# Second attention's sums: four engines in written order, its token states made beside the scans, routing cut into stages

## The chip, the core and the metric

The kernel runs on one core of a Trainium2 chip. A core has five engines that run side by side, each through its own queue in order: PE (TensorE, matrix products into PSUM), DVE (VectorE), ACT (ScalarE), POOL (GpSimd, which also issues the indirect DMAs here) and SP (which issues other DMAs). They wait for each other through semaphores. The metric is the device time of one execution in microseconds; lower is better.

## What is computed

Four layers work on an image of 256 channels and 64x64 points. Layers 0 and 1 are a windowed linear attention and a deformable convolution. The change is in layer 2, which sees the image as 4096 tokens of 256 channels: a gated linear attention over the tokens with 8 heads of 32 channels, and then a mixture of experts in which each token goes to its two best of eight. Layer 3 has a softmax attention and another such mixture. What matters of layer 2, cut:

```python
t = t + _L2_attn_ref(_ln_t(t), ...)
t = t + _L2_ffn_ref(_ln_t(t), ...)

# in _L2_attn_ref
sim = jnp.einsum('bhld,bhld->bhl', q, k) * qk_norm_scale
k = _l2_normalize(k)
v = _l2_normalize(v)
Z = jnp.einsum('bhld,bhle->bhlde', v, k) * kv_norm_scale
gates_logits = jnp.einsum('bhli,oi->bhlo', gate_inputs, wg_w) + wg_b
gates = jnp.square(jax.nn.relu(gates_logits)) + EPS
m_scan, s_scan = _online_softmax_scan(sim)
Z_scan = jnp.cumsum(gates[..., None] * Z, axis=2)
g_scan = jnp.cumsum(gates[..., None], axis=2)
softmax_weights = (jnp.exp(sim - m_scan) / (s_scan + EPS))[..., None, None]
attn_weights = Z_scan / (g_scan + EPS) * (1.0 + jax.nn.silu(softmax_weights))
ctxt = jnp.einsum('bhld,bhlde->bhle', q, attn_weights)
return _linear(ctxt, wo_w, wo_b)

# in _moe, on the normalized tokens
probs = jax.nn.softmax(tokens @ router_w.T, axis=-1)
rw, re = jax.lax.top_k(probs, TOP_K)
```

## The kernel before

All is in 32-bit floats, and the 4096 tokens are 32 tiles of 128 (`NT`; `P` is 128, `C` 256, `D` 32, `NB` 512, `TPB` 4). `attn2` holds queries and keys in `A["qk"]`, values in `A["v"]` and their transposes in `A["vT"]`, and goes through three stages.

**Projections** (`attn2_project`): layer norm, queries, keys and values, gates, and keys scaled by their gates (L1507 on POOL), block by block of four tiles.

**Scans** (`attn2_fac`): the running sums and maxima along the tokens, as one factor per token and head. They are a chain of small steps on DVE and ACT; `carry` twice sends ends of segments through PE (`c8`, then `back`). They end in `A["fac"]`.

**Sums** (`attn2_sum`): 16 slots of two tiles. In slot u, `turn(u+1)` transposes the next scaled queries (PSUM tag "o", copied to `qT` by ACT), `states(u)` makes the products of values and keys of its two tiles (128x128 each, of which the 32x32 blocks on the diagonal are used) and adds them to the running state on DVE, `out(u-1)` multiplies the context by the output weights (tag "o" too) and adds it to the tokens `t` on DVE, `context(u)` adds what earlier tiles give (`earlier`, L1655, with the state) and what the tile itself gives (`within`, L1661), and `scores(u+1)` makes the next scores, which DVE masks with the triangle (L1631). `scale(u)` on POOL multiplies the queries by the factor and adds the bias `wo_b` to the tokens (L1609, L1610).

Between these, every second slot starts `route` for four finished tiles, a generator in five pieces: layer norm; transposes; the second transposes and t = t (1 + r) + shift on ACT (L1970); logits, the two best experts (`top2`) and counts; places and eight scatters (L2006, indirect DMAs on POOL, one for each tile and rank) of the normalized rows into the experts' lists `xs` in DRAM. After the last of them `tile_table` works out which expert each tile of the lists belongs to, and `expert_tiles` loads weights and rows (L2095 to L2102).

The order: in the sums only PE's order is as written (`manual_schedule` with PE alone). Those of DVE, ACT and POOL are set when the program is built, by a planner that follows priorities and its own idea of when each input is there; so the 16 additions of L1610 run during the projections already, and the 16 of L1609 at the start of the sums. In the scans the planner sets all engines. The square root in `layer_norm` (L204) and the exponential in `top2` (L1941) use different tables of ACT, which loads a table ahead of the first function that needs another one.

## Time and profile before

| what | us |
|---|---|
| median of 10 runs | 3437.05 (3431.53 to 3440.94) |
| profiled execution | 3435.9 |
| its span, first to last instruction | 3433.7 |
| mean granted clock of PE | 0.955 |
| projections of layer 2 | 1436 to 1567 |
| scans | 1567 to 1586 |
| sums: first scaled query to end of the last context | 1586.0 to 1725.2 |
| last scatter issued | 1757.3 |
| first load of expert weights | 1760.3 |

Times in the trace count from the span's start. A group's row gives busy time and mean length of one instruction, and then how long the engine was idle just before it, with what released it. In the timeline, a row merges equal instructions that follow each other, and stands at the start of the first.

In the projections DVE is busy 119.3 of 131 us and PE 117.0. From 1763 on the experts follow, and then layer 3, which ends at 3433.7; the change leaves their code as it is.

### The profile page before, as it was taken

Reading aid. Unit: us, or ns where it says so; the run is one execution under the profiler, and the core shown is the slowest. Engines: PE = TensorE matmul, PEld = TensorE weight load, DVE = VectorE, ACT = ScalarE, POOL = GpSimd, SP = SyncE. Lnnn points to the kernel's source line nnn. Section 1 sums busy time; section 2 is a strip of 40 time slices with the busy share of each in tenths; the row PEclk is TensorE's granted clock in tenths of the full one; section 3 lists DMA queues with packets and bytes.
Section 4 is the critical chain, followed back from the end, with each engine's and each line's share of the span. In section 5 each row is a group of like instructions: output and inputs, shape, how many; then the busy total and the mean of one; then the engine's idle time right before and its main releaser. Section 6 shows DMA issues by size and latency. Waiting matters only on the chain.

```text
span 3433.7 us, 65430 instructions
## 1 busy us (share of the span) xinstructions
PE 3100.0 (90%) x25404; PEld 2322.7 (68%) x25404; DVE 2309.3 (67%) x5378; ACT 1318.8 (38%) x2538; POOL 1448.4 (42%) x1293
## 2 busy tenths in 40 slices
PE   6779999999977899897969699999999996999997
PEld 3443444344435888665857468888888885989896
DVE  8885677577754677797755576777777775555552
ACT  4444344444425666243533352222222222333331
POOL 2028788788833555343444352000000003555552
PEclk9889999999989999898979899999999997999998
DMA  2145556521133222100158643322333314555554
GB/s 72 42 115 144 161 155 168 127 68 52 49 119 109 68 71 73 47 1 1 63 178 267 216 181 120 102 89 93 99 99 101 96 56 160 194 196 208 202 202 175
DMA packets 241686, 406.97 MB, mean 119 GB/s; under 512 B 78353, under 2 KB 152850, under 8 KB 231890
## 3 DMA queue, kind: packets, MB, share of 16 engines
q1 hardware_dynamic: 212002, 344.40, 32.2%
q0 software_dynamic: 13056, 35.93, 2.8%
q10 hardware_dynamic: 16304, 22.31, 1.9%
q8 instruction: 204, 3.34, 0.4%
q14 instruction: 120, 0.98, 0.1%
HBM read 287.07 MB, written 111.30 MB: 116 GB/s over the span
## 4 chain that ended last, share of the span: by engine, by line
PE 41%; DVE 9%; DMA 5%; issue 5%; ACT 3%; POOL 3%; SPq 0%; DVEq 0%; POOLq 0%; ACTq 0%
PE a_sa_ps L2438 6%; PE f_h_ps L146 5%; DMA ys<-f_y,f_at 3%; PE l_acc_ps L1132 3%; PE a_oa_ps L2477 3%; PE a_ob_ps L2477 3%; PE a_oc_ps L2477 3%; PE a_sb_ps L2438 3%; PE f_ya_ps L146 2%; PE f_yb_ps L146 2%; DVE l_pr L1128 2%; PE a_od_ps L2477 1%; POOL ys L2193 1%; PE a_sc_ps L2438 1%; PE a_q_ps L146 1%
## 5 line engine op out<-in xcount | busy, mean ns | idle before, releaser
L748 ACT COPY l_sc<-l_s 128x384 f32<-128x384 f32 (+1 forms) x632 | 303.9, 532 | 454.3 <-PE l_s L741 448.0
L753 DVE TENSOR_TENSOR l_sm<-l_s,mask 128x256 f32<-128x256 f32 (+2 forms) x628 | 308.0, 551 | 91.7 <-PE l_s L741 90.6
L2006 POOL DMA_INDIRECT xs<-f_room,f_to x64 | 64.7, 1012 | 696.7 <-issue 581.5
L146 PE MATMUL f_h_ps<-f_xT,f_w 128*128 128x256 f32 x1440 | 340.7, 387 | 18.9 <-DVE f_xT L2113 9.5
L146 PEld LDWEIGHTS f_h_ps<-f_xT,f_w 128*128 128x128 f32 x1440 | 262.1, 192 | 82.8 <-ACT f_h L2123 31.5
L741 PE MATMUL l_s<-l_q,l_k 32*128 32x256 f32 (+3 forms) x2944 | 270.5, 453 | 0.0
L2457 ACT ACTIVATE a_e<-a_e 128x512 f32<-128x512 f32 x256 | 155.8, 629 | 242.3 <-DVE a_e L2427 241.3
L758 POOL TENSOR_TENSOR l_sm<-l_sc,mask 128x768 f32<-128x768 f32 (+1 forms) x116 | 203.0, 1758 | 88.1 <-ACT l_sc L748 87.9
L2123 ACT ACTIVATE f_h<-f_h_ps,f_w 128x256 f32<-128x256 f32 x360 | 166.4, 470 | 187.6 <-PE f_h_ps L146 178.0
L1128 DVE TENSOR_TENSOR l_pr<-l_vk,l_w_ps 128x1280 f32<-128x1280 f32 x128 | 186.6, 1481 | 56.9 <-PE l_acc_ps L1132 38.4
L741 PEld LDWEIGHTS l_s<-l_q,l_k 32*128 32x128 f32 x2944 | 132.4, 183 | 115.2 <-issue 67.2
L1132 PE MATMUL l_acc_ps<-ident,l_pr 128*128 128x128 f32 x1600 | 198.8, 278 | 7.7 <-POOL l_pr L1123 7.6
L2193 POOL DMA_INDIRECT ys<-f_y,f_at x144 | 145.8, 1013 | 138.1 <-ACT f_y L2192 108.0
L1132 PEld LDWEIGHTS l_acc_ps<-ident,l_pr 128*128 128x128 f32 x1600 | 185.3, 144 | 14.2 <-POOL l_pr L1123 8.6
L762 POOL TENSOR_TENSOR l_sm<-l_sc,mask 128x256 f32<-128x256 f32 (+1 forms) x220 | 185.2, 871 | 14.1 <-ACT l_sc L748 13.3
L2150 POOL TENSOR_TENSOR f_wt<-f_w 128x512 f32<-128x512 f32 x72 | 90.0, 1270 | 218.5 <-PE f_ya_ps L146 207.1
L2438 PE MATMUL a_sa_ps<-a_q,a_kt 128*128 128x256 f32 x512 | 155.9, 386 | 13.7 <-DVE a_u L2443 12.9
L2442 ACT COPY a_u<-a_sa_ps 128x256 f32<-128x256 f32 x128 | 47.6, 372 | 293.4 <-PE a_sa_ps L2438 293.4
L787 PE MATMUL l_b_ps<-l_sm,l_v 128*32 128x256 f32 (+2 forms) x2176 | 153.7, 372 | 0.0
L2438 PE MATMUL a_sa_ps<-a_qt,a_kt 128*128 128x256 f32 x512 | 153.1, 381 | 0.0
L758 POOL TENSOR_TENSOR l_sm<-l_sc,mask_c 128x768 f32<-128x768 f32 (+1 forms) x64 | 120.9, 1905 | 40.4 <-ACT l_sc L748 39.9
L2438 PE MATMUL a_sb_ps<-a_qt,a_kt 128*128 128x256 f32 x512 | 131.4, 379 | 0.0
(559 smaller groups left out, 7274.9 us busy)
## 6 DMA issues: line engine op xcount, KB each, us to landing
a_kt<-a_kd SPq DMA_DIRECT2D x128, 512.0 KB
f_w<-in_f_w SPq DMA_DIRECT2D x36, 1152.0 KB
f_w<-in_f_w SPq DMA_DIRECT2D x36, 1028.0 KB
xs<-zero SPq DMA_DIRECT2D x8, 4160.0 KB
l_vk<-vt SPq DMA_DIRECT2D x180, 128.0 KB
f_x<-xs SPq DMA_DIRECT2D x72, 260.0 KB
f_w<-in_f_w SPq DMA_DIRECT2D x36, 384.0 KB
l_rcp<-l_recd SPq DMA_DIRECT2D x48, 256.0 KB
```

What stands on the lines that cost most here:

```text
L146: self.nc.tensor.matmul(out, lhsT, rhs, start=(i == 0), stop=(i == len(pairs) - 1))
L741: nc.tensor.matmul(s[pair, j][:, at : at + m, :], key(hp), qs[hp], start=(z == 0), stop=(z == len(pieces) - 1))
L748: nc.scalar.copy(sc[:, j], s[1, j])
L753: nc.vector.tensor_tensor(to(pair, j, kind, at), pick(s[pair, j], kind, which), mask, ALU.mult)
L758: nc.gpsimd.tensor_tensor(out[:, :, at, :], of[:, :, which, :], bc(mask, 1, 2), ALU.mult)
L762: nc.gpsimd.tensor_tensor(to(1, j, kind, at), pick(sc[:, j], kind, which), mask, ALU.mult)
L1128: nc.vector.tensor_tensor(pr, vk, bc(held["w"][:, j, dy], 3, D), ALU.mult)
L1132: nc.tensor.matmul(acc[:, m, j, :], pf[:, dx, m * P : (m + 1) * P], self.ident, is_transpose=True, start=(j == 0 and dy == 0 and dx == 0 a ...
L2123: nc.scalar.activation(h[:, m, :], q, AF.Gelu, bias=w1[:, 2 * hidden + m : 2 * hidden + m + 1])
L2193: nc.gpsimd.indirect_dma_start(out=self.ys_parts[(i % 4) * NI + k], in_=y[:, k, :], in_offset=None, out_offset=bass.IndirectOffsetOnAxis(a ...
L2438: mm = lambda out, i, right: nc.tensor.matmul(out, A[i], right, start=True, stop=True)
L2477: nc.tensor.matmul(out, vs[:, j, i, :], right, start=(j == 0 and side != 1), stop=(j == NPAIR - 1 and side != 0))
```

## The change

The token states go from the sums to the scans. `attn2_states` makes, for each of the first 31 tiles, eight products of 128x32 by 128x32 (four heads in each half), so that only the 32x32 blocks are made; ACT copies four tiles at a time from PSUM to `A["st"]`, and POOL adds them up one after the other. `beside(n)` writes n tiles of these ahead of PE's `c8`, `back` and last transposes in the scans (8, 1, 12, 1 and the remaining 9 tiles). The scans are reordered: the running maximum and its exponentials come ahead of the sum of the gates, and the reciprocal of that sum is written at the end.

In the scans and in the sums PE, DVE, ACT and POOL now all run in written order. `scale` and the addition of `wo_b` are two steps, `scale(u+2)` and `bias(u+1)` of a slot. `route` is cut into 14 named steps by `route_parts` (`norm_parts` cuts the layer norm); for the sums `do(u, late, name)` writes a step `late` slots after that in which its group's last tiles are finished, and scatters go out four to a slot. The last four tiles are two groups of two. The transposed queries and the context lie in the projection weights' room `w_qkv2`, whose use is over, the triangle is made before the projections, and the PSUM bank of the states becomes one for logits and places ("few"). The steps of routing themselves are the same as before; `route` for layer 3 runs them in its old order.

```diff
@@ -1361,6 +1383,7 @@
+            tri = self.triangle(pool)
...
+            left = ExitStack()
+            A["st"] = left.enter_context(tc.tile_pool(name="a2s", bufs=1)).tile([P, NT, 2, D], F32, tag="st", name="a2_st")
             self.attn2_fac(A)
...
-                bank = lambda: ps.tile([P, NB], F32, tag="r", name="f_r_ps")
+                bank = lambda few=False: ps.tile([P, TPB * NE if few else NB], F32, tag="few" if few else "r", name="f_r_ps")
...
-                    return self.route(t0, T, t, S, wp, n.rearrange("p (i c) -> p i c", c=CX), nT, bank)
-                self.attn2_sum(t, A, ked, wp, ps, route)
+                    return self.route_parts(t0, T, t, S, wp, n.rearrange("p (i c) -> p i c", c=CX), nT, bank)
+                self.attn2_sum(t, A, tri, ked, wp, ps, route)
+    def attn2_states(self, A, ps):
+        nc = self.nc
+        st, banks = A["st"], []
+        def product(ti):
+            if ti % 8 == 0:
+                banks.append(ps.tile([P, 8, 2, D], F32, tag=f"st{ti // 8}", name="a2_st_ps"))
+            for m in range(2):
+                for h in range(4):
+                    hp, at = slice(h * D, (h + 1) * D), slice(m * P + h * D, m * P + (h + 1) * D)
+                    nc.tensor.matmul(banks[-1][hp, ti % 8, m, :], A["v"][:, ti, at], A["qk"][:, ti, C + at.start : C + at.stop], start=True, stop=True)
+            if ti % 4 == 3 or ti == NT - 2:
+                lo = ti // 4 * 4
+                nc.scalar.copy(st[:, lo + 1 : ti + 2], banks[-1][:, lo % 8 : ti % 8 + 1])
+                for i in range(max(1, lo), ti + 1):
+                    nc.gpsimd.tensor_tensor(st[:, i + 1], st[:, i + 1], st[:, i], ALU.add)
+        return [(lambda ti: lambda: product(ti))(ti) for ti in range(NT - 1)]
     def attn2_fac(self, A):
...
+            tc.manual_schedule(engines={ET.PE, ET.DVE, ET.Activation, ET.Pool}),
...
+            states = self.attn2_states(A, ps)
+            def beside(n):
+                for go in states[:n]:
+                    go()
+                del states[:n]
...
+            def carry(ends, scan, first, fill):
...
                 p = ps.tile([NH, len(ends), NS], F32, tag="c8", name="a2_c8")
+                beside(fill)
                 self.mm(p.rearrange("p j s -> p (j s)"), [(hot, R.rearrange("p j s -> p (j s)"))])
...
                 p = ps.tile([P, len(first), NS], F32, tag="back", name="a2_back")
+                beside(1)
                 self.mm(p, [(hotT, x[:, :, 0:NS])])
...
-            c2 = carry([ends[:, 0:1], ends[:, 1:2]], sums_and_tops, (0.0, -3e38))
+            c2 = carry([ends[:, 0:1], ends[:, 1:2]], sums_and_tops, (0.0, -3e38), 8)
+            mx = pool.tile([P, L + 1], F32, tag="mx", name="a2_mx")
+            nc.vector.tensor_copy(mx[:, 0:1], c2[:, 1:2])
+            nc.vector.tensor_tensor_scan(mx[:, 1:], s, s, c2[:, 1:2], ALU.max, ALU.max)
+            far = pool.tile([P, L], F32, tag="far", name="a2_far")
+            nc.scalar.activation(far, mx[:, 1:], AF.Exp, scale=-1.0, bias=c2[:, 1:2])
+            nc.vector.tensor_sub(s, s, mx[:, 1:])
+            nc.scalar.activation(s, s, AF.Exp)
+            dec = pool.tile([P, L], F32, tag="dec", name="a2_dec")
+            nc.vector.tensor_sub(dec, mx[:, :L], mx[:, 1:])
+            nc.scalar.activation(dec, dec, AF.Exp)
             gs = pool.tile([P, L], F32, tag="gs", name="a2_gs")
             nc.vector.tensor_tensor_scan(gs, one.to_broadcast([P, L]), g, c2[:, 0:1], ALU.mult, ALU.add)
             nc.vector.tensor_scalar_add(gs, gs, 1e-5)
-            mx = pool.tile([P, L + 1], F32, tag="mx", name="a2_mx")
-            nc.vector.tensor_copy(mx[:, 0:1], c2[:, 1:2])
-            nc.vector.tensor_tensor_scan(mx[:, 1:], s, s, c2[:, 1:2], ALU.max, ALU.max)
-            nc.vector.tensor_sub(s, s, mx[:, 1:])
-            dec = pool.tile([P, L], F32, tag="dec", name="a2_dec")
-            nc.vector.tensor_sub(dec, mx[:, :L], mx[:, 1:])
-            far = pool.tile([P, L], F32, tag="far", name="a2_far")
-            nc.scalar.activation(s, s, AF.Exp)
-            nc.scalar.activation(dec, dec, AF.Exp)
-            nc.scalar.activation(far, mx[:, 1:], AF.Exp, scale=-1.0, bias=c2[:, 1:2])
             tot = pool.tile([P, L], F32, tag="tot", name="a2_tot")
             nc.vector.tensor_tensor_scan(tot, dec, s, 0.0, ALU.mult, ALU.add)
             c1 = carry([tot[:, L - 1 : L], far[:, L - 1 : L]],
                        lambda x, c: nc.vector.tensor_tensor_scan(x[:, 0, :], c[:, 1, :], c[:, 0, :], 0.0, ALU.mult, ALU.add),
-                       (0.0,))
+                       (0.0,), 12)
...
             nc.vector.reciprocal(gs, gs)
             nc.vector.scalar_tensor_tensor(s, s, 1.0, gs, ALU.add, ALU.mult)
+            beside(len(states))
             p = ps.tile([P, 2, P], F32, tag="fac", name="a2_fac_ps")
...
-    def attn2_sum(self, t, A, ked, wp, ps, route):
+    def attn2_sum(self, t, A, tri, ked, wp, ps, route):
...
-        tri = self.triangle(wp)
-        qTs, sms, before, cTs = {}, {}, {}, {}
+        ET = mybir.EngineType
+        U = NT // 2
+        qTs, sms, cTs, R = {}, {}, {}, {}
+        room = lambda i: w["w_qkv2"].rearrange("p k n -> p (k n)")[:, i * NB : (i + 1) * NB].rearrange("p (m j n) -> p m j n", m=2, j=2)
         two = lambda u: slice(2 * u, 2 * u + 2)
         keys = lambda ti: A["qk"][:, ti, C:]
         def scale(u):
             qh = A["qk"][:, two(u), 0:C].rearrange("p t (h d) -> p t h d", d=D)
             nc.gpsimd.tensor_tensor(qh, qh, bc(A["fac"][:, :, u, :], 3, D), ALU.mult)
+        def bias(u):
             nc.gpsimd.tensor_tensor(t[:, two(u), :], t[:, two(u), :], bc(self.row("wo_b"), 1, 2), ALU.add)
...
-            qTs[u] = wp.tile([P, 2, 2, P], F32, tag="qT", name="a2_qT")
+            qTs[u] = room(u % 2)
...
-        def states(u):
...
-                        nc.tensor.matmul(c[hp, m, j, :], before[2 * u + j][hp, m, hp], qTs[u][hp, m, j, :], start=(first and m == 0), stop=False)
+                        nc.tensor.matmul(c[hp, m, j, :], A["st"][hp, 2 * u + j, m, :], qTs[u][hp, m, j, :], start=(first and m == 0), stop=False)
...
-            cTs[u] = wp.tile([P, 2, 2, P], F32, tag="cT", name="a2_cT")
+            cTs[u] = room(2)
...
-        steps = []
...
-        with self.tc.manual_schedule(engines={mybir.EngineType.PE}):
-            scale(0)
-            scale(1)
+        groups = [(2 * r + 2, 4 * r, 4) for r in range(U // 2 - 1)] + [(U - 1, NT - 4, 2), (U, NT - 2, 2)]
+        def do(u, late, name, *args, only=(4, 2)):
+            for at, t0, T in groups:
+                if at + late == u and T in only:
+                    if t0 not in R:
+                        R[t0] = route(t0, T)
+                    if args and isinstance(args[0], slice):
+                        R[t0][name](range(T)[args[0]])
+                    else:
+                        R[t0][name](*args)
+        every, fore, hind = slice(None), slice(0, 2), slice(2, 4)
+        with self.tc.manual_schedule(engines={ET.PE, ET.DVE, ET.Activation, ET.Pool}):
+            for u in range(2):
+                scale(u)
+            bias(0)
             turn(0)
             scores(0)
-            for u in range(U + 1):
+            for u in range(U + 7):
+                if u + 1 < U:
+                    turn(u + 1)
+                do(u, 1, "norm")
+                do(u, 2, "turn", 1)
+                do(u, 4, "find")
+                do(u, 4, "weigh")
+                do(u, 4, "scatter", fore)
                 if u + 2 < U:
                     scale(u + 2)
+                do(u, 5, "scatter", hind)
                 if u + 1 < U:
-                    turn(u + 1)
-                if u < U:
-                    states(u)
-                if u > 0:
+                    bias(u + 1)
+                do(u, 3, "top")
+                do(u, 3, "count")
+                if 0 < u <= U:
                     out(u - 1)
-                step()
-                if u > 0 and u % 2 == 0:
-                    steps.append(route(2 * u - 4, TPB))
+                do(u, -1, "stats", fore, only=(4,))
+                do(u, 0, "stats", hind, only=(4,))
+                do(u, 0, "stats", every, only=(2,))
+                do(u, 2, "move", every)
+                do(u, 0, "root")
+                do(u, 1, "turn", 0)
+                do(u, 0, "scales")
                 if u < U:
                     context(u)
                 if u + 1 < U:
                     scores(u + 1)
-                step()
-            while steps:
-                step()
+                do(u, 3, "exp")
+                do(u, 2, "logits")
+                do(u, 3, "place")
...
-        nc.scalar.activation(e, e, AF.Exp)
-        one = pool.tile([P, TPB], F32, tag="f_w1", name="top_w1", bufs=1)[:, :T]
-        nc.vector.tensor_scalar_add(one, e, 1.0)
-        nc.vector.reciprocal(w[:, 0], one)
-        nc.vector.tensor_mul(w[:, 1], e, w[:, 0])
+        def weigh():
+            one = pool.tile([P, TPB], F32, tag="f_w1", name="top_w1", bufs=1)[:, :T]
+            nc.vector.tensor_scalar_add(one, e, 1.0)
+            nc.vector.reciprocal(w[:, 0], one)
+            nc.vector.tensor_mul(w[:, 1], e, w[:, 0])
+        return (lambda: nc.scalar.activation(e, e, AF.Exp)), weigh
...
+        def move(which):
+            if L == 2:
+                r = got["r"]
+                if which[0] == 0:
+                    nc.vector.tensor_scalar_add(r, r, 1.0)
+                for i in which:
+                    nc.scalar.activation(t[:, t0 + i, :], t[:, t0 + i, :], AF.Identity, bias=got["shift"][:, i : i + 1], scale=r[:, i : i + 1])
...
+        def scatter(which):
+            for i in which:
+                for r in range(2):
+                    nc.gpsimd.indirect_dma_start(
+                        out=self.xs_parts[(2 * (t0 + i) + r) % (4 * TPB)], in_=n[:, i, :], in_offset=None,
+                        out_offset=bass.IndirectOffsetOnAxis(ap=S["to"][:, r, t0 + i : t0 + i + 1], axis=0),
+                    )
```

## The prediction

> **What bounds the kernel now.** The change lies between the end of the second attention's projections and the first load of its experts. I read first the busy time by stage, for the scans, one pair of slots of the sums, and the tail (columns: stretch, its length, busy time and instruction count of PE, weight load, DVE, ACT and POOL, granted clock, DMA share, GB/s):
>
> ```profile
> 1567.00:1586.00 19.00, 3.53 (x14) 2.24 (x14) 12.69 (x37) 4.15 (x7) 2.63 (x4) 0.50 0.00 0
> 1661.74:1679.62 17.88, 17.23 (x261) 15.27 (x260) 13.85 (x50) 10.11 (x19) 7.91 (x9) 1.00 0.17 62
> 1728.00:1760.00 32.00, 10.62 (x49) 8.94 (x49) 18.48 (x99) 6.53 (x13) 20.29 (x21) 0.55 0.25 92
> ```
>
> The scans are a chain on DVE with PE nearly free. In the sums PE works 17.23 of 17.88 us: it sets the pace. In the tail no compute engine is full; POOL's scatters end it. Then the groups of the sums (busy and mean, then idle before and its releaser), for what goes and what will stand in a queue:
>
> ```profile
> L146 PE MATMUL a_st_ps<-a_qk,a_v 128*128 128x128 f32 x128 | 17.8, 285 | 0.0
> L1645 DVE TENSOR_TENSOR a_before<-a_before,a_st_ps 128x256 f32<-128x256 f32 x30 | 12.4, 414 | 0.3
> L1970 ACT ACTIVATE t<-t,ln_shift,ln_rstd 128x256 f32<-128x256 f32 x32 | 16.8, 590 | 9.6 <-DVE ln_rstd L1968 9.6
> L204 ACT ACT_TABLE_LOAD x7 | 9.0, 1283 | 0.1
> L2006 POOL DMA_INDIRECT xs<-a_qk,f_to x64 | 62.0, 968 | 63.1 <-ACT t L1970 36.7 <-issue 16.5 <-DVE t L1680 7.2
> ```
>
> Last the timeline, for what waits on what (start, length, instruction):
>
> ```profile
> 1628.48 1.28 ACT L1941 ACT_TABLE_LOAD   x1
> 1629.77 0.21 ACT L1941 ACTIVATE top_e<-top_e 128x4 f32<-128x4 f32 x1
> ...
> 1669.77 0.16 DVE L2003 CAST f_to<-f_place 128x8 int32<-128x8 f32 x1
> 1670.04 2.07 ACT L1970 ACTIVATE t<-t,ln_shift,ln_rstd 128x256 f32<-128x256 f32 x4 [1.86 <-DVE ln_rstd L1968]
> ...
> 1670.80 0.98 POOL L2006 DMA_INDIRECT xs<-a_qk,f_to  x1 [6.95 <-ACT t L1970]
> 1672.09 0.96 POOL L2006 DMA_INDIRECT xs<-a_qk,f_to  x1 [0.31 <-issue]
> ...
> 1736.41 0.96 POOL L2006 DMA_INDIRECT xs<-a_qk,f_to  x1 [2.30 <-ACT t L1970]
> 1757.30 0.96 POOL L2006 DMA_INDIRECT xs<-a_qk,f_to  x1 [0.30 <-issue]
> 1760.26 0.37 SPq L2100 DMA_DIRECT2D f_w<-in_f_w  x1
> ```
>
> Three things: a function of another table costs 1.28 us on ACT before it starts; a scatter starts 0.87 us after its places are cast (1670.80 less 1669.93; 1748.38 less 1747.51 likewise), and scatters follow at 1.267 us; experts load only when the last scatter has landed (2.4 us after its start). "ACT t" as releaser is a coincidence, since a scatter does not read t.
>
> **Scans and start.** The 248 products of 128x32 stand before PE's waits for DVE. The row nearest in form (L1661, 128x32 weights) goes at 37 ns in the first, half-clock slot: 64 products 2.4 us, 96 products 3.6, 72 products 2.7, against waits of 3.5, 5.7 and 4.5 us. So nothing on the path; at twice the pitch some 1.7 us. On DVE the maximum scan goes ahead of the sum scan, which starts ACT 0.6 us earlier; but the reciprocal of gs (1.74 us), now in a gap, stands behind the last product and beside a Silu of 0.42: +0.75. The eight copies of 128x256 fit on ACT (0.45 each by L1674), but the last three stand behind that Silu, and behind them 11 additions of 128x64 on POOL, then scale(0). No row shows such an addition: the 128x4 copy is 0.19 us, the 128x128 addition 0.54. Between them, by columns, 0.31; last copies start 1584.2, so POOL is free at 1587.6, not 1586.0: **+1.6 us** (ends: 0.4 less and 3.4 more; and 1.6 less if the scans' first tile no longer waits for POOL, a wait of 2.1 us at 1567 that other addresses may end).
>
> The Trainium skill (GPSIMD Engine Reference, Engine selection) gives elementwise additions to VectorE as about twice as fast; it speaks against moving these to POOL. By half of 0.31 the start would lose 1.6 less; no run here shows the pair of shapes.
>
> **Slots 0 to 3** (little routing). Products leave PE: 1.9 us in a cold slot, 0.95 in a warm one. But they stood between turn(u+1) and out(u-1), which share the PSUM bank "o", and covered ACT's copy of it. PE now waits 0.85 (0.66 to the last transpose, 0.57 copy, hand-offs, less 0.46 issue). Warm slots: 1.62 out + 2.0 context + 1.65 scores + 0.46 + 0.85 = 6.6 for 6.98. Cold start 0.25, slot 0 1.3, then three times 0.4: **-2.75** (a further 3.2 less if the products keep the clock up; the clock was 0.5 until 1596.)
>
> **Slots 4 to 15.** If PE set the pace, a pair would take 15.1 (two turns 0.92, outs 3.24, contexts 4.0, scores 3.3, four-transposes 0.92, logits 2.0, place 0.6) and waits of 1.65 for qT: 16.75. Two loops are longer.
>
> *DVE in written order.* Odd slot: logits copy 0.22, top-2 2.47 (1742.61 to 1745.08, dependent steps of 0.22), counts 1.1, add 0.72, two tiles of statistics 1.1, two masks 2.28: 7.9. Even slot: copy of turn(1) 0.6, find and weigh 1.4, add 0.72, statistics 1.1, r+1 and eps 0.25, scales 0.32, masks 2.28: 6.7. Between eps and scales it waits for Sqrt, which on ACT now stands behind move's four: 0.2 + 2.07 + 1.28 + 0.20 + 0.05, less the 0.25 counted: 3.55. Behind it wait both masks, and so the next context and top-2. Sum **18.15**.
>
> *POOL and PE.* Four scatters of an even slot stand before scale(u+2). Weigh to scatter 0.87, four 5.07, scale 1.05, transposes 0.66, qT 0.57, out 1.62, four-transposes 0.46, context 2.0, scores to last mask 3.56, copy 0.6, find 0.85, weigh 0.57, ten hand-offs 0.4: **18.3**.
>
> Both above 17.88. First pair (no scatters) 16.7 for 18.4, -1.7; four pairs at 18.3, +1.7; the last as before: **0** (ends: -1.13 each for six pairs, -6.8, were neither loop closed; +3 if a hand-off is 0.08, not 0.04).
>
> The wo_b additions (16 of 1.09), so far among the projections, now stand on POOL behind hind scatters: per pair 10.1 + 2.1 + 2.2 + 0.2 = 14.7, covered by 18.3, seen only where PE or DVE fell under 15.
>
> The skill's ScalarE: Activation LUTs (What ACT_TABLE_LOAD costs) adds a drain of 1.38 to 1.28. Here the next activation starts 0.01 us after the load (1629.77), so no drain. By the page a pair would be 19.5 and the sum below some 7 us more.
>
> **Tail**, from the end of context(15), C = 1725.2 before. Before, the eight scatters of tiles 24-27 start at C+11.2, the last of all ends at C+33.05. Afterwards their find and weigh stand two slots later, behind in DVE's order: counts, add, statistics of tiles 28-29, root: 3.8; copy and transposes 1.25, copy 0.7, find, weigh 1.5, add 0.7, statistics 1.1, eps 0.25 (9.3); the Sqrt wait 3.55, scales, logits copy 0.55; turn 1.1, top-2 and counts 3.6, next logits 0.35, ACT and half-clock transposes 2.0, copy 0.35, find and weigh 1.5: C+22.2. Then 0.87, 16 scatters 20.3 and a gap 0.3: C+43.5, against 33.05: **+10.4**. Lower end: POOL never starves and the last 24 scatters run from C+2.9: C+33.3, nothing. With only the find of tiles 20-23 late (C+7.7) it is +5. Upper: +12. The table of tiles on DVE (8.4 us after the last find at C+33) ends just before the scatters.
>
> **Sum.** 1.6 - 2.75 + 0 + 10.4 = +9.25 on the profiled execution: 3435.9 to 3445 (span 3433.7). The median shown is 1.15 above that execution: 3437.05 + 9.25 = **3446**.
>
> **Rivals.**
> *PE keeps the pace* (for it: PE 17.23 of 17.88, 17.8 us removed; against: the two loops). Pairs 16.75, tail +0.2: 1.6 - 2.75 - 6.8 + 0.2 = -7.75, 3429. Faster. It decides where Sqrt is asked for early enough and scale is not held.
> *Tail held by POOL alone*: as forecast with tail +5 (for it: POOL 20.29 of 32 in the tail; against: short slots are still chains on DVE): +3.85, 3441, no change.
> *More is cut off by order*: POOL additions of 0.54 (+1.8 more), hand-offs (+3), tail +12: 1.6 + 1.8 - 2.75 + 3 + 12 = +15.65, 3453. For it: 0.87 before a scatter; against: rows measured idle.
> *Clock kept by the products*: 3.2 off the forecast, 3443, still inside no change; PE is idle 4 us between bursts, and only 7 us of unbroken work raised the clock at 1596.
>
> **How the numbers follow.** Forecast 0.42, PE's pace 0.18, POOL tail 0.18, more cut off 0.12, clock 0.10. The median cannot tell less than 0.2% (6.9 us) from no change: faster below 3430.2, slower above 3443.9. Slower: 0.42 + 0.12 = 0.54. No change: 0.18 + 0.10 and a quarter of PE's case: 0.32. Faster 0.14. The range leaves out half of PE's case and the top of the worst: 3430 to 3454; the forecast's own range is 3442 to 3451.
>
> **What would show it.** Right: in a pair DVE idle some 3.5 us before the reciprocal of ln_rstd, released by ACT; transposes of the query released by POOL's scale; pairs near 18.3; scatters of tiles 24-27 starting 20 us or more after the last context. Wrong: pairs under 17, PE idle only for qT; Sqrt before move; eight scatters started within 12 us of that context; scale(0) before 1586 after the scans' start at 1567. A clock of 1.0 right after the scans would make slots 0 and 1 wrong. Rows shifted ahead of 1567 would mean the projections moved, which I price at nothing: DVE is their bound and waited for POOL 0.9 us there.

## The result, and the profile after

The change made the kernel slower: 3472.52 us (median of 9 runs, 3466.97 to 3477.92) against 3437.32 us, a ratio of 1.0103 (95% interval 1.0094 to 1.0112). The forecast was 3446 us with a range up to 3454. The profiled execution took 3475.62 us (span 3473.9).

In the table, "rows" is PE's first transpose of the scans, "turn 0" its first transpose of a query, C the end of the last context's products. In the tables, and wherever a slot's time or clock is given, slot u runs from PE's transposes of query u to those of the next, so slot 4 begins at turn 4 (in the program `turn(4)` is the first step of slot 3). A pair is the mean over slots 7 to 14. All come from the timelines of PE and POOL.

| stretch | before | forecast | after |
|---|---|---|---|
| rows to turn 0 | 20.0 us | +1.6 | 23.6 us: +3.6 |
| slots 0 to 3 | 25.05 us | -2.75 | 24.65 us: -0.4 |
| slot 4 to C | 113.0 us | 0 | 129.9 us: +16.9 |
| (a pair in it) | 17.88 us | 18.3 us | 21.97 us |
| C to the end of the last scatter | 33.0 us | +10.4 | 43.9 us: +10.9 |
| sum | | +9.25 | +31.0 |

The tail is near the forecast and the start 2 us off; the sums are far from it. First the busy time by stage of the kernel after: scans, one pair of slots, tail (columns as in the forecast):

```profile
1567.00:1588.00 21.00, 11.53 (x510) 9.58 (x510) 13.39 (x36) 6.97 (x15) 10.58 (x28) 0.50 0.01 4
1673.75:1695.88 22.13, 18.95 (x245) 15.41 (x245) 17.67 (x47) 10.45 (x19) 12.11 (x14) 0.81 0.14 50
1748.00:1793.00 45.00, 15.07 (x66) 12.86 (x66) 24.36 (x138) 14.49 (x28) 23.67 (x25) 0.55 0.20 72
```

Two things in the second line were not in the forecast. PE has fewer instructions than before (245 for 261 matmuls) and is busy for longer (18.95 us for 17.23), because its granted clock is 0.81 where it was 1.00. And DVE, with 47 instructions for 50, is busy for 17.67 us where it was 13.85. The groups of the kernel after say which instruction of DVE grew:

```profile
L1674 POOL TENSOR_TENSOR t<-t,pr 128x512 f32<-128x512 f32 x16 | 17.5, 1096 | 0.1
L1671 POOL TENSOR_TENSOR a_qk<-a_qk,a_fac 128x512 f32<-128x512 f32 x16 | 16.8, 1050 | 0.1
L225 DVE SCALAR_TENSOR_TENSOR ln_shift<-ln_mv,ln_rstd 128x4 f32<-128x4 f32 x15 | 15.1, 1012 | 0.4
```

`ln_shift` multiplies two tensors of 128x4: a mean of 1012 ns over its 15 calls, 8 of them in the projections; the 7 in the sums have a mean of 1986 ns. In the timeline of the kernel before, the same instruction and `f_hot`, which also has two inputs in SBUF, take:

```profile
1664.72 0.19 DVE L1932 TENSOR_TENSOR f_hot<-top_key,top_first 128x32 f32<-128x32 f32 x1
1665.27 0.16 DVE L208 SCALAR_TENSOR_TENSOR ln_shift<-ln_mv,ln_rstd 128x4 f32<-128x4 f32 x1
```

The timeline of the kernel after, cut to DVE, POOL and PE around one `ln_shift` and one `f_hot`:

```profile
1672.54 0.18 DVE L222 RECIPROCAL ln_rstd<-ln_rstd 128x4 f32<-128x4 f32 x1 [3.57 <-ACT ln_rstd L218]
1672.63 1.06 POOL L1671 TENSOR_TENSOR a_qk<-a_qk,a_fac 128x512 f32<-128x512 f32 x1
1672.75 3.14 DVE L225 SCALAR_TENSOR_TENSOR ln_shift<-ln_mv,ln_rstd 128x4 f32<-128x4 f32 x1
1673.63 1.10 POOL L1674 TENSOR_TENSOR t<-t,pr 128x512 f32<-128x512 f32 x1
1673.75 1.11 PE L1680 MATMUL a_qT_ps<-ident,a_qk 128*128 128x128 f32 x4 [3.07 <-POOL a_qk L1671]
1674.66 0.20 POOL L2050 COPY a_qk<-out_row 128x4 f32<-128x4 f32 x1
1674.81 1.05 POOL L1671 TENSOR_TENSOR a_qk<-a_qk,a_fac 128x512 f32<-128x512 f32 x1
1675.54 3.78 PE L146 MATMUL a_o_ps<-w_o,w_qkv 128*128 128x256 f32 x8 [0.68 <-ACT w_qkv L1682]
1675.81 2.34 DVE L1695 TENSOR_TENSOR a_sm<-a_s,tri 128x1024 f32<-128x1024 f32 x2
...
1680.38 0.19 DVE L2002 TENSOR_REDUCE top_first<-top_key 128x4 f32<-128x32 f32 x1
1680.60 1.44 DVE L2003 TENSOR_TENSOR f_hot<-top_key,top_first 128x32 f32<-128x32 f32 x1
1680.88 1.10 POOL L1674 TENSOR_TENSOR t<-t,pr 128x512 f32<-128x512 f32 x1
```

Read the ends. `ln_shift` begins at 1672.75 and ends at 1675.89; POOL's scale, bias addition, copy and next scale run without a gap from 1672.63 to 1675.86. `f_hot`, 0.19 us elsewhere, ends at 1682.04, 0.06 after the addition beside it. The masks, whose scores lie in PSUM, keep their length beside POOL's scales (2.35 us at 1601.16 in the kernel after, 2.36 in the one before). What is stretched has two inputs in SBUF. That is theory H: DVE is held while POOL's elementwise work runs, 3.0 us in an even slot of the program and 1.25 us in an odd one. The waits that the forecast did name are all there: 3.57 us for Sqrt, 3.07 us of PE for POOL's scale, 0.68 us for the copied query. PE's out, 1.99 us at full clock, takes 3.78 us.

The Trainium skill (SBUF — State Buffer, SBUF: two separate sides) states the rule: VectorE and GpSimd share a pair of ports, which one of them has for its whole instruction, and a VectorE instruction with two SBUF inputs needs it against a GpSimd one that reads SBUF. The trace agrees in the ends (0.06 us or less between them), and adds that DVE did not get in between four POOL instructions that followed each other. In the starts it doesn't show the rule: by the page whichever starts first has the ports, and the record of `f_hot` starts 0.28 us before that of the addition, at its usual 0.19 us early enough to be over. Why it was held is open.

### The profile page after: what moved, and what is told of

Read it like the earlier page. It is cut to its first block, busy times and chain, and to the rows that moved or that the text cites. A ratio compares the mean times of both kernels' runs of the same rounds, so it can differ in the third digit from the quotient of the medians.

```text
span 3473.9 us, 66259 instructions
## 1 busy us (share of the span) xinstructions
PE 3119.2 (90%) x25776; PEld 2330.1 (67%) x25776; DVE 2327.7 (67%) x5375; ACT 1322.8 (38%) x2549; POOL 1458.8 (42%) x1324
## 4 chain that ended last, share of the span: by engine, by line
PE 40%; DVE 11%; DMA 5%; issue 5%; ACT 3%; POOL 3%; SPq 0%; POOLq 0%; DVEq 0%; ACTq 0%
PE a_sa_ps L2544 6%; PE f_h_ps L146 5%; PE l_acc_ps L1154 3%; PE a_oa_ps L2583 3%; PE a_ob_ps L2583 3%; PE a_oc_ps L2583 3%; DMA ys<-f_y,f_at 3%; PE a_sb_ps L2544 3%; PE f_ya_ps L146 2%; PE f_yb_ps L146 2%; POOL ys L2299 1%; DVE l_pr L1150 1%; PE a_od_ps L2583 1%; PE a_qkv_ps L146 1%; PE a_q_ps L146 1%
## 5 line engine op out<-in xcount | busy, mean ns | idle before, releaser
L763 PEld LDWEIGHTS l_s<-l_q,l_k 32*128 32x128 f32 x2944 | 132.3, 183 | 115.2 <-issue 67.5
```

The lines of the kernel that those rows point to most:

```text
L763: nc.tensor.matmul(s[pair, j][:, at : at + m, :], key(hp), qs[hp], start=(z == 0), stop=(z == len(pieces) - 1))
```

## The experiments

The runs fell on six chips. On four, before takes 3434 to 3438 us; on the other two, with runs 1 to 4 and 12 to 15, it takes 3506 and 3497 us, and PE there stands idle with "issue" as releaser beside the scatters. On these two odd chips only the lengths of single instructions are read; sizes come from the other four. Six of the eight kernels that ran there took less time than before on the same chip (ratios 0.9925 to 0.9977; runs 2 and 15 took 1.0001 and 1.0009). The kernel after itself did not run there, so whether the change as it stands costs time on such a chip isn't known. Two rivals stand against H. Theory S: POOL's scatters and the scale behind them set the pair. Theory C: the clock, which the removed products had kept up.

| run (chips that feed PE) | ratio, 95% interval | pair | slot 4 to C |
|---|---|---|---|
| e6 after again | 1.0120 (1.0103 to 1.0136) | 21.99 | 129.9 |
| e18 bias additions early | 1.0076 (1.0062 to 1.0090) | 20.64 | 124.9 |
| e9 ln_shift on ACT | 1.0085 (1.0059 to 1.0112) | 20.50 | 128.6 |
| e8 additions and scales early | 1.0041 (1.0028 to 1.0054) | 18.87 | 117.8 |
| e7 e8 and Sqrt first | 1.0051 (1.0034 to 1.0068) | 18.80 | 115.2 |
| e10 e7 and PE kept busy | 1.0007 (0.9996 to 1.0018) | 17.20 | 106.9 |
| e11 e10 and a new tail | 0.9988 (0.9974 to 1.0003) | 17.20 | 106.9 |
| e16 e11 and a new start | 1.0005 (0.9996 to 1.0014) | 16.86 | 108.6 |

**Runs 1, 13 and 18: the bias additions out of the slots.** They go ahead of the scans in the program, and the planner puts them among the projections, where they were before the change.

```
+            for u in range(NT // 2):
+                two = slice(2 * u, 2 * u + 2)
+                nc.gpsimd.tensor_tensor(t[:, two, :], t[:, two, :], bc(self.row("wo_b"), 1, 2), ALU.add)
             left = ExitStack()
...
-            bias(0)
...
-                if u + 1 < U:
-                    bias(u + 1)
```

> Theory H (a DVE instruction with two SBUF inputs is held for as long as POOL's elementwise additions and products run, and these holds, 3.0 us in an even slot and 1.25 us in an odd one, lengthen DVE's written order from 18.1 to 22.1 us a pair): with the 16 wo_b additions among the projections, as before the change, the hold of f_hot goes (-1.25) and the hold of ln_shift shrinks by one addition (-1.05): pairs of 19.8 us, six pairs -14 us, 3458 us. Theory S (the pair is paced by POOL's scatters and the scale queued behind them; the stretched DVE instruction only fills a wait that DVE would have had anyway): the additions stand behind the scale, so pairs stay at 22 us and the time at 3472 us, less 2 us at the end.

> The kernel of the first run once more, on a chip that feeds PE: only the 16 wo_b additions are taken out of the slots, which the forecast had called covered by the pair of 18.3 us. If they were covered: pairs of 22 us, ratio 1.010. Theory H: f_hot is not held (0.19 us for 1.44) and ln_shift one addition less (2.1 us for 3.2): pairs of 19.8 us, ratio 1.006 to 1.007.

> The kernel of the first and the thirteenth run a last time: only the 16 wo_b additions are out of the slots, the scales stay behind the scatters. On a chip that feeds PE: if the additions were covered, as forecast, pairs of 22 us and ratio 1.010; by theory H pairs of 19.8 us and ratio 1.006 to 1.007. On a chip that starves PE: pairs of 24 to 26 us again, and nothing follows.

Runs 1 and 13 fell on the two odd chips (ratios 0.9962 and 0.9977, pairs of 25.3 and 24.4 us with some 16 and 9 us of "issue" in the sums): no size can be read, though `f_hot` took 0.19 us and `ln_shift`, where it was held, 1.97 to 2.14 in both. Run 18, on a chip that feeds PE, has the same lengths and a pair of 20.64 us, 1.3 less than after. So the additions, called covered in the forecast, were not. But it is 20.6, not 19.8: something else sets the pair then. Its timeline points to what:

```profile
1670.78 1.06 POOL L1674 TENSOR_TENSOR a_qk<-a_qk,a_fac 128x512 f32<-128x512 f32 x1
1671.02 1.97 DVE L225 SCALAR_TENSOR_TENSOR ln_shift<-ln_mv,ln_rstd 128x4 f32<-128x4 f32 x1
1671.89 1.11 PE L1683 MATMUL a_qT_ps<-ident,a_qk 128*128 128x128 f32 x4 [1.24 <-POOL a_qk L1674]
1673.68 3.78 PE L146 MATMUL a_o_ps<-w_o,w_qkv 128*128 128x256 f32 x8 [0.68 <-ACT w_qkv L1685]
```

PE waits for the scale behind the scatters, and then goes on at half rate (transposes 1.11 us for 0.63, out 3.78 for 1.99). That is the forecast's second loop, with PE's part of it 2.9 us dearer than it was priced (18.3 and 2.9 would be 21.2; the 0.6 us that the pair is shorter aren't accounted for).

**Runs 4 and 9: ln_shift on ACT.** POOL's work is untouched; five small activations take the place of one DVE instruction.

```
-            if on_act:
+            if on_act and by_act:
+                for i in range(n):
+                    nc.scalar.activation(shift[:, i : i + 1], mv[:, i, 0:1], AF.Identity, scale=r[:, i : i + 1])
+                nc.scalar.activation(shift, shift, AF.Identity, scale=-1.0)
+            elif on_act:
                 nc.vector.scalar_tensor_tensor(shift, mv[:, :, 0], -1.0, r, ALU.mult, ALU.mult)
```

> ln_shift of the routing is made by five small activations on ACT (about 1 us) in place of one DVE instruction with two SBUF inputs; POOL's work is untouched. Theory H: the hold of 3.0 us goes from DVE's order, the masks behind it start at once; the hold of f_hot stays: pairs of 19.1 us, six pairs -18 us, 3454 us. Theory S: DVE waits the same 3 us somewhere else, pairs stay at 22 us: 3472 us.

> The kernel of the fourth run once more, for the same reason: ln_shift made on ACT, POOL's work untouched. Theory H: the 3.0 us hold goes from DVE's order, the masks start when the scores are there: pairs of 19 us, six pairs -15 to -18 us, ratio to before 1.007. Theory S: pairs stay at 22 us, ratio 1.012.

Run 9: pairs of 20.5 us, and `f_hot` is 0.19 us again, since the additions now run beside other instructions (`top_key<-f_lg,top_m` takes 0.45 to 0.63 us for 0.19). Run 4, on an odd chip, had 24.9 us and `top_key<-top_rest,top_m` held instead, three times for 1.42 to 1.45 us. Without touching POOL, moving one instruction of 128x4 is worth 1.5 us a pair: theory S alone, which said no gain, falls. H said 19.1 us; the pair stops at the same 20.5 as in run 18, the loop by the scale.

**Runs 2 and 8: scales early too**, all 16 at the start of the sums, so that in the slots POOL has small copies and scatters only.

```
-            for u in range(2):
+            for u in range(U):
                 scale(u)
...
-                if u + 2 < U:
-                    scale(u + 2)
```

> As the run before, and all 16 scales at the start of the sums: in the slots POOL has scatters and small copies alone. Theory H: no DVE instruction is held, pairs are DVE's 18.1 us with its wait of 3.6 us for Sqrt still in, six pairs -24 us: 3448 us. Theory S: the scale is out of the way of the scatters too, and DVE's wait for Sqrt is what is left: also 18.1 us and 3448 us. A pair above 20 us would speak against both.

> The kernel of the second run once more, hoping for a chip that does not starve PE of instructions. Theory H: no DVE instruction with two SBUF inputs is stretched (ln_shift 0.16 us, f_hot 0.19); DVE's written order with the wait of 3.6 us for Sqrt is 18.1 us, against 22.1 in the kernel after: six pairs -20 to -24 us, ratio to before 1.005 to 1.007. If Sqrt's wait adds to what the run with Sqrt first had (pairs of 18.8 us, ratio 1.005), pairs of 20 us or more, ratio 1.008. If PE shows 'issue' in its idle time, the sizes say nothing and only the stretched instructions count.

No DVE instruction is held in either (`ln_shift` 0.16 us every time). Run 8 has pairs of 18.87 us and 1.0041. It can't tell H from S: with the scales gone from behind the scatters PE's wait for them is gone too, as are the holds. The busy time of one of its pairs:

```profile
1656.54:1675.01 18.47, 17.16 (x247) 14.30 (x246) 13.65 (x46) 10.41 (x20) 8.24 (x10) 0.91 0.19 65
```

DVE is back at 13.65 us; PE fills the pair, at a clock of 0.91. Run 2, the same kernel on an odd chip, took 28.15 us a pair with some 22 us of "issue".

**Runs 3 and 7: Sqrt ahead of move**, alone and with the additions and scales early.

```
+                if u < U:
+                    do(u, 0, "root")
                 do(u, 2, "move", every)
-                do(u, 0, "root")
+                if u >= U:
+                    do(u, 0, "root")
```

> Sqrt is asked for ahead of the four activations of move (up to slot 15). Theory H: DVE's wait of 3.6 us goes, and ln_shift runs before POOL comes to its scale, so its hold of 3.0 us goes too; what is left is the loop by weigh, scatters, scale and transposes, 18.3 us: six pairs -23 us, 3449 us. Theory S: the scale behind the scatters still sets the pair, DVE waits elsewhere: pairs of 21 to 22 us, 3466 to 3472 us.

> The additions and scales early, as in the second run, and Sqrt asked for ahead of move. Theory H with DVE's wait of 3.6 us also gone: DVE needs 14.6 us a pair, PE 16.8: pairs of 17 us, six pairs -30 us against the kernel after (ratio to before 1.000 with the tail still +10). Theory F: the eight scatters stand back to back, PE is starved for 4 to 8 us in each even slot, pairs of 24 us or more as in the second run.

Run 3 (odd chip, 25.6 us a pair) shows only that `ln_shift` then is 0.16 us, since it runs before POOL comes to the scale. Run 7 takes the 3.57 us wait out of run 8's kernel (DVE waits 0.23 us for Sqrt): pairs of 18.80 us for 18.87, and the intervals overlap. Once POOL's work is gone, the wait for Sqrt costs next to nothing in the pairs; DVE had that time to spare.

**Run 10: PE kept busy.** Products that nobody reads, in the context's PSUM tile ahead of its first real product, where the states' products stood before the change.

```
+            for _ in range(times):
+                nc.tensor.matmul(cs[u][:, 0, 0, :], self.ident, tri, start=True, stop=True)
...
+            warm(0, 6)
             turn(0)
+            warm(0, 3)
             scores(0)
...
                     turn(u + 1)
+                if u < U and (u < 6 or u % 2):
+                    warm(u, 3)
```

> As the run with additions, scales and Sqrt early (pairs of 18.8 us, ratio 1.005), and PE is given work that nobody reads where the states' products stood before the change: three 128x128 products behind turn(u+1) in odd slots and in slots 0 to 5, nine before the first scores. Theory C (the wait of 0.7 us for the copy of the query, which the states' products covered, lets the granted clock fall to half; outs of 3.8 us for 2.0, pairs 1.5 us longer): granted clock 1.00 in slots 4 to 15, pairs of 17.5 us, first slots 2 us shorter: -10 us, ratio 1.002. Rival (DVE and POOL set the pair, the clock follows from PE's waiting): pairs stay at 18.8, the added products cost up to 5 us: ratio 1.005 to 1.0065.

```profile
1685.20:1701.96 16.76, 16.52 (x252) 14.15 (x252) 13.95 (x47) 10.27 (x19) 8.17 (x10) 0.98 0.19 65
```

More instructions, less time: clock 0.98 in this pair, PE busy 16.52 us for 17.16 in run 8, slots 0 to 3 in 22.6 us for 28.7 in run 7, ratio 1.0007 for 1.0051 in run 7 (another chip) and 1.0041 in run 8 (the same one). Against run 7 the edit leaves DVE and POOL alone, so the clock is a cause here, not a sign of their waits: theory C's forecast came in, in the main. It was worth 1.6 us a pair. What it was worth in the first slots is less sure: the kernel of runs 1, 13 and 18 took 24.4, 25.4 and 28.4 us for them, so without added products the clock rises sooner or later from one execution to another, and the gain is 2 to 6 us. In some slots the clock still fell (0.81, 9.2 us for 7.8), so three products are barely enough.

That the length of a wait decides is not shown. In run 7 PE waits in a pair 0.68 and 0.24 us, and the clock of every second slot is 0.68 or 0.82; the kernel before waits 0.65 us in every pair (for the copied query, at 1668.22 for instance) and keeps 1.00. What the record shows is that similar waits with less work between them lost the clock, and added work brought it back.

**Run 11: another tail.** Behind the last context, tiles 20 to 23 scatter at once, and tiles 24 to 27 go through logits, top-2, places and scatters ahead of the two groups of two; the moves stand last.

> As the run before, and behind the last context the stages of the last three groups stand in an order of their own: the eight scatters of tiles 20 to 23 at once, then tiles 24 to 27 through logits, top-2 and scatter ahead of the two groups of two. Theory T (the tail is a chain in DVE's written order, POOL starves for want of places): the last scatter ends at 33 to 35 us behind the end of the last context, as before the change, in place of 44: -9 us, ratio 0.9995. If the tail is POOL's 24 scatters alone, nothing is gained: ratio 1.002.

The last scatter ends at C+35.9 for C+40.7 in run 10: 4.8 us of the 9 expected. The eight scatters of tiles 20 to 23 still began only at C+5.3, because their weights wait 1.55 us for an Exp that stands behind the context's copies on ACT.

**Run 12: the busy PE alone**, on the kernel after.

> The kernel after with nothing moved, and PE's unread products of the tenth run added. The fourth corner of the square: holds and clock loss together 22.1 us a pair, no holds but clock loss 18.8, neither 16.9. If holds and clock add up: pairs of 20.2 us, ratio to before 1.007. If POOL's holds alone set the pair and the clock only follows from PE's waits: clock still under 1.0 in slots 5 to 14, pairs of 21.5 to 22 us, only the first slots shorter, ratio 1.009 to 1.010.

It fell on an odd chip: pairs of 23.9 us, clock 0.72 to 0.83 in slots 7 to 14, `ln_shift` 2.98 to 3.17 us long. With 7.2 us of "issue" in PE, which may lower the clock too, it can't say whether holds and clock add up. That is open.

**Runs 14 to 16: a better start and tail**: the last 15 additions of the states behind the first scales, and fewer products ahead of the second carries; in run 15 also Exp, places and scatters of tiles 20 to 23 inside slot 15.

```
-                       (0.0,), 12)
+                       (0.0,), 7, 0)
...
             for u in range(U):
                 scale(u)
+                if u >= 3 and A["late"]:
+                    A["late"].pop(0)()
```

> The eleventh kernel (0.9988), with the start mended: the last 15 additions of the states stand on POOL behind the first scales, and 7 products, not 13, stand ahead of the second scans' carries. By the traces DVE waits 1.49 and 1.28 us there for 0.45 and 0.69 before the change, and the first scale waits 1.7 us for POOL: the first scale 3.3 us earlier, ratio 0.9978.

> As the run before, and in slot 15 the Exp, places, find and weigh of tiles 20 to 23 stand ahead of the last two outs, so that their scatters need not wait 1.55 us for Exp behind the context's copy and POOL doesn't stand idle for 5 us: first scatter behind the last context 3 us earlier; the last group's places and the table of tiles then set the end: 1 to 2 us, ratio 0.9973.

> The kernel of the fourteenth run once more. On a chip that feeds PE (before at 3437 us): pairs of 16.9 us as in the tenth and eleventh runs, the first scale 3.3 us earlier than in the eleventh: ratio to before 0.9978. On a chip that starves PE (before at 3500 us): ratio 0.9976 again.

Run 16 shows a miss of mine: DVE's waits at the carries shrank as wanted (0.45 and 0.70 us), but the products moved back now stood ahead of the transposes of the factor, where PE waited 0.49 us for a copy on ACT and 0.86 us more for nothing that the profile shows. In its timeline:

```profile
1588.31 0.74 PE L1555 MATMUL a_st_ps<-a_qk,a_v 128*32 128x32 f32 x34 [0.86 <-issue]
1588.99 0.69 PE L1660 MATMUL a_fac_ps<-ident,a_gs__17354 128*128 128x128 f32 x2
1589.71 0.42 DVE L1661 COPY a_fac<-a_fac_ps 128x256 f32<-128x256 f32 x1 [3.70 <-PE a_fac_ps L1660]
```

DVE waits 3.70 us there for 0.79 after the change, and rows to turn 0 takes 24.8 us. Nothing was gained: 1.0005. Run 15 (odd chip, 1.0009) was slower than run 14 beside it (0.9976).

**Runs 5, 6 and 17: both kernels unchanged.**

> The kernel before, unchanged, for its trace beside the others of this call. If the chip of the four earlier runs is slower for every kernel by the clock, the time between the stages is stretched evenly; if it starves PE of instructions while scatters run, its trace shows PE idle with 'issue' as releaser in the sums (none in the first trace of before) and a pair of more than 17.9 us.

> The kernel after, unchanged, beside the same runs of before. Theory H: POOL's holds are there on any chip, pairs of 22 us where PE is not starved; ratio 1.010 to before. If PE is starved of instructions while scatters stand back to back (theory F, from the traces of the four earlier runs: 9 to 22 us of 'issue' in PE's idle time, none in the first trace of after), pairs are 24 us and more on such a chip, and the ratio depends on the chip.

> The kernel before, unchanged, for its trace on the same chip. On a chip that starves PE, where before takes 3500 us: if the loss lies in the sums too, PE shows 'issue' as releaser of idle time there, for some 60 us, more than in the changed kernels (7 to 20 us), and the way behind the first load of the experts stays at 1672 us. On a chip that feeds PE: 3437 us, none.

All three fell on chips that feed PE, with no "issue" in the sums. Before has 17.87 or 17.88 us a pair in all three traces, after 21.97 and 21.99 in both. No trace of before from an odd chip was had. None of the versions is measurably faster than before where PE is fed: run 11's interval, 0.9974 to 1.0003, holds 1.

## Why the prediction was wrong

**The sign was right, the size was not**: +9.25 us forecast, +31.0 us measured from the scans to the last scatter in the first pair of traces. The sign is not luck, since the tail that carried it came out as priced; but over half of the loss lies in a term that was put at 0.

**The step that failed is "Slots 4 to 15", the sum "0"**: 18.15 and 18.3 us for its two loops, measured 21.97 a pair.

- *DVE in written order, 18.15 us.* Its parts are right (the Sqrt wait 3.57 for 3.55, the masks 2.34 for 2.28). What was left out are the holds: 18.15 + 3.0 + 1.25 = 22.4, close to 21.97. The sentence that did it is that the wo_b additions were "covered by 18.3": time on POOL was counted as if it cost no other engine anything. Taking only the additions away gave 1.3 us a pair back (run 18), taking one held instruction away 1.5 (run 9), taking all of POOL's elementwise work out of the slots 3.1 (run 8, which also ends PE's wait for the scale). How much of the 21.97 is hold and how much clock stays open, since run 12 couldn't tell.
- *POOL and PE, 18.3 us.* The loop is there and sets the pair in runs 9 and 18, but at 20.5 us, since its transposes, out and four-transposes were priced at full clock and run at half: 1.11 for 0.66, 3.6 for 1.62, 1.0 for 0.46, together +2.9 us (0.7 us more than the loop measured). The 1.62 was too little at full clock as well: from its start to the next instruction's an out takes 1.8 to 1.9 us in the trace before.
- With no hold and little clock loss the pair is 16.9 to 17.2 us (runs 16 and 10); where the clock stays at 1.00 throughout, two slots take 16.5. The forecast's rival "PE keeps the pace" said 16.75. It asked for Sqrt early and scale not held; it also needed something for PE to do while it waits for the copied query.

**The row was there to be seen.** In the projections of the kernel before, `a_g<-a_g,a_r`, 128x32, takes 1.96 us at 1489.53, beside a POOL product of 2.35, and 0.17 us at 1494.93, with POOL idle. The timeline of the kernel before, cut:

```profile
1489.09 2.35 POOL L1476 TENSOR_TENSOR a_room<-a_qk 128x1024 f32<-128x1024 f32 x1 [1.23 <-DVE a_g L1500]
1489.53 1.96 DVE L1501 TENSOR_TENSOR a_g<-a_g,a_r 128x32 f32<-128x32 f32 x1
...
1494.93 0.17 DVE L1506 TENSOR_TENSOR a_g<-a_g,a_r 128x32 f32<-128x32 f32 x1
```

I read only POOL's side, a constant 1.05 us for its scales, and concluded that the two don't disturb each other.

**Slots 0 to 3**, -2.75: measured -0.4 up to turn 4, and -1.3 (32.1 us for 33.4) up to turn 5, where the forecast's slot 3 ends. The products did leave PE. The slot that was to lose 1.3 us lost 0.25: its clock was 0.70 for 0.78 before. The next two ran at a clock of 1.00 and took 6.98 and 6.92 us for 6.98: PE was busy for 6.25 us of them and waited 0.7 for the copied query, and the out took 1.93 us from start to start, before as after, where the sum has 1.62. So the time of the products came back as a wait. Run 10 (with the scales early too) is 2.4 us shorter than before in these slots, all of it in the first two, at a clock of 0.93 and 1.00 for 0.50 and 0.78: that is the unread products ahead of the first scores, not the missing ones. The rival "clock kept by the products" looked at what the scans' products might add, not at what the missing ones take away.

**Scans and start**, +1.6: measured +3.6. Of the 2.0 us between them, 0.9 are POOL's last 11 additions: 4.34 us in a row, 0.39 from one to the next, where the sum has 3.4. One takes 0.32 us, about as estimated, but the time between them was left out (and 0.31 was low for its two rows, 0.19 and 0.54, which give 0.36 at 64 columns). The other 1.1 us are the later start of these additions, 1585.46 for 1584.2, by the 248 products, priced at "nothing on the path". The timeline of the kernel after, cut to these waits and the end:

```profile
1578.77 0.44 PE L1551 MATMUL a_st_ps<-a_qk,a_v 128*32 128x32 f32 x16 [0.49 <-ACT a_st L1554]
1579.33 0.18 DVE L1601 COPY a_c<-a_c 8x32 f32<-8x32 f32 x1 [1.50 <-PE a_c L146]
1581.13 0.17 DVE L1610 TENSOR_TENSOR a_z<-a_back,a_seg 128x16 f32<-128x16 f32 x1 [1.30 <-PE a_back L146]
1585.46 4.34 POOL L1556 TENSOR_TENSOR a_st<-a_st 128x64 f32<-128x64 f32 x11 [4.09 <-ACT a_st L1554]
1586.37 0.48 DVE L1649 SCALAR_TENSOR_TENSOR a_gs__17338<-a_gs__17338,a_gs 128x256 f32<-128x256 f32 x1
1589.76 2.05 POOL L1671 TENSOR_TENSOR a_qk<-a_qk,a_fac 128x512 f32<-128x512 f32 x2
```

DVE's two waits were 0.45 and 0.69 us before: +1.66, of which the new order of the scans wins a part back. The products fit PE's time, but they wait for ACT to empty their PSUM banks between its exponentials, and the carries queue behind them.

**Tail**, +10.4 to C+43.5: measured C+43.9, by the steps given. Run 11 supports its cause: another written order takes 4.8 us off.

**ACT's table load** came without a drain here too (next activation 0.01 us after it), so the 18.15 stood without the Trainium skill's 1.38 us (ScalarE: Activation LUTs).

**Left open.** Of the 40 us between the first two spans, 9 lie behind the first load of the experts' rows. That stretch takes 1672.0, 1677.1 and 1675.5 us in three traces of before and 1680.9 and 1679.8 in two of after, but 1671.7 to 1678.9 in the other kernels on chips that feed PE. I don't know whether any of it belongs to the change.

## What to carry to other kernels

Before moving elementwise work to POOL, or into a stretch where DVE runs small steps in a chain, list DVE's instructions with two SBUF inputs there: each can cost as much as the POOL work that it meets, however small it is, and where POOL's instructions follow each other without a gap, as much as several of them. Removing PE work from a stretch that PE fills can make the rest of it slower; ask which wait the removed work covered and whether the granted clock holds without it, and price the next products at both rates. When one loop is shortened, the next one is close: here 22.0, 20.5, 18.8 and 17.2 us came off one after the other, each with another cause.

## What the runs showed that was not expected

**On two chips PE ran out of instructions, as it seems.** The kernels of runs 14 and 16 are the same. PE's waits in the sums in run 14:

```profile
PE a_s L1699 <- issue: 12.1, 30, 0.9
PE f_r_ps L146 <- issue: 4.8, 10, 0.8
```

In run 16 no "issue" appears there at all, and the pair is 16.86 us for 26.43. In run 2 each of the 45 such gaps lies while scatters run or within 2 us of them. That scatters and the fetching of instructions are in each other's way is argued from this, not shown.

**Less work, lower clock.** The kernel before has 261 matmuls in a pair and a clock of 1.00. Run 8, in which PE waits for no scale, has 247 and 0.91 in the pair shown; run 10, with three unread products in every second slot, 252 and 0.98. In the kernel after the clock of a pair is 0.81, and there the wait of 3.07 us for POOL's scale may have a part in it.

**POOL did not let DVE in between, without gaps.** One DVE instruction of 0.16 us was held through four POOL instructions in a row, 3.14 us, though each of them ended in between. These followed each other without a gap (each record starts before the last one ends). In the scans it was otherwise: POOL's 11 additions of 0.32 us stand 0.39 apart, and DVE's 128x256 instruction at 1586.37, which has two SBUF inputs as well, took 0.48 us among them for 0.42 before, while the addition beside it took 0.38. Beside DVE's scan at 1576.48 (0.82 us for 0.69 before) one took 0.58. So DVE got in there, and POOL's additions waited. That the gap decides is likely from these rows, and not tested.
